# A mixture-of-experts tail whose weights are loaded once, kept in SBUF and copied to each tile by VectorE

## Chip, core and metric

The kernel runs on one core of one Trainium2 chip. The metric is the device time of one execution in microseconds (us), the median of three runs. The core's engines are named as in the profile: PE (TensorE matmuls), PEld (TensorE weight loads), DVE (VectorE), ACT (ScalarE), POOL (GpSimd), SP (SyncE, which here only issues DMAs).

## What is computed

Two layers of a hybrid vision network on an input of 2 images of 56 x 56 positions and 256 channels, all in float32. Layer 0 is a neighbourhood attention (7 x 7 window, 8 heads) behind a group norm. Layer 1 is a gated linear attention over the 3136 tokens of each image, followed by a mixture of experts. The mixture is the part that the change touches:

```python
xf = x.reshape(-1, 256)                          # 6272 tokens
probs = softmax(xf @ gate_w + gate_b)            # 8 experts
top2_vals, top2_idx = top_k(probs, 2)
cw = zeros((N, 8)); cw[arange(N)[:, None], top2_idx] += top2_vals
for e in range(8):                               # W1: 256 x 512, W2: 512 x 256
    h = gelu(xf @ W1[e] + b1[e])
    out += cw[:, e, None] * (h @ W2[e] + b2[e])
```

The kernel does not run every expert on every token. It sorts the 2 x 6272 pairs of token and expert by expert and runs each expert on its own tokens alone.

## The kernel before, in words

**Steps.** Layer 1 goes through the tokens in 13 steps (`NS1`) of 256 tokens of each image; the last step has 64. Three generators make a step: `before(s)` (projections and gates), `attention(s)` and, one step later, `route(s)`. `route(s)` normalises the result, computes the gate, finds each token's two experts and the slot of each pair, and scatters the token's row (256 channels, its number and its gate weights) into the DRAM buffer `xs_d`, which has one region per expert. It ends with `listed(s)`, which turns the counts into a list of full tiles: for each place its first row in `xs_d` and its expert, written as integers to a small tile `ent`. `together(main, *others)` interleaves the turns of these generators by fixed proportions.

**Places.** A place is one tile of slots of one expert. There are 57 of them (`NP`): 48 large ones of 256 slots and 9 small ones of 128. The first 41 (`sure1(NS1 - 2)`) are known to be full before the last step is routed. The last 16 are known only once `listed(NS1)` has run behind the last step; `places()` orders them as small and large in turn: S L S L S S L S L S S L S L S L. For each place `experts()` does the following.

- `fetch`: SP reads the place's row and expert from `ent` into registers (L1482), loads the slots `xg` from `xs_d` (L1492) and the expert's weights `wj` (128 partitions x 2308 floats, L1501) from DRAM.
- `gather`: DVE makes the row indices (`rowk`, L1514) and the gate weight of each slot (`cws`, L1522); PE transposes the slots (L1535), ACT copies them out (L1539).
- `hidden`: PE makes the hidden layer (`p_h`, L1550), ACT applies the gelu (`hT`, L1557).
- `results`: ACT writes the weighted bias to `ye` (L1569), PE makes the result (`p_y`, L1575), DVE adds the weighted result to `ye` (L1582), and POOL issues one indirect DMA per 128 slots that adds `ye` to the rows of `out` (L1585). Two places can hold rows of one token, so each place's adds wait until those of the place before have landed:

```python
before_it = added[-1] if added else []
...
waits_for(add, *before_it)
```

**Order.** In the steps the places run as one of the `others` of `together`, up to a bound `upto_k`; whatever is left runs behind the steps, in what is called the tail here. `ask` keeps the fetches ahead of the computing. In the steps a place's `xg` and `wj` lie in the pool `fw` of four buffers. When the steps' pools have been closed, the tail opens a second pool `tw` of four on their memory, uses both in turns of four, and lets the fetches run up to five places ahead. `fy` holds six buffers of `ye`. Within the order of priority the compiler places each engine's instructions by its own schedule, so that instructions of several generators stand mixed on an engine, and each engine then works through its own list in order.

Of the kernel before, what the change touches and what calls it, by code (L numbers as in the profile page):

```python
# [15 lines left out]
F32 = mybir.dt.float32  # L16
# [8 lines left out]
P = 128  # L25
# [23 lines left out]
NE, FF = 8, 512  # L49
# [8 lines left out]
RG = NB * L + SL  # L58
# [6 lines left out]
NS1 = -(-L // B1)  # L65
WJ = NG * FF + NF * C + NF + C
WP = 4
FW = 4
NW = 48
NO = 52  # L70
NP = 57
# [5 lines left out]
    return W, T, W // T  # L77


def places():  # L80

    first = sure1(NS1 - 2)
    large, small = iter(range(first, NW)), iter(range(NW, NP))
    return [*range(first), *(next(small if h else large) for h in (1, 0, 1, 0, 1, 1, 0, 1, 0, 1, 1, 0, 1, 0, 1, 0))]


def assigned(s):
    return 2 * NB * min((s + 1) * B1, L)


def sure1(s):
    return max(0, -((NE * (SL - 1) - assigned(s)) // SL))
# [717 lines left out]
def layer1(tc, t, out, x1_d, xs_d, ident, load, K, plain, lx, last_rows, lite):  # L810
    nc = tc.nc
# [11 lines left out]
    with ExitStack() as whole:  # L823
# [16 lines left out]
            pool = use.late if use.late is not None and n % 2 else p1  # L840
            return pool.tile(shape, F32, tag=tag, name=tag)

        use = SimpleNamespace(ahead=2, asked=0, tail=None, late=None)
        xin = {}

        def load_x(s):
# [17 lines left out]
        for what, shape, value in (  # L864
# [4 lines left out]
            first = const.tile(shape, F32, name=f"first_{what}")  # L869
# [575 lines left out]
        entry, added, puts, stores = [], [], {}, {}  # L1445
        fetched = {}
        order = places()
# [4 lines left out]
        def parts(k):  # L1452
            return 2 if order[k] < NW else 1

        def filled_at(k):
            return next((s for s in range(NS1) if sure1(s) > order[k]), NS1)

        def blank():
            for e in range(NE):
                row = nc.values_load(  # L1460
                    behind_[0:1, e : e + 1],
                    engines=[mybir.EngineType.SP],
                    min_val=e * RG,
                    max_val=e * RG + NB * L,
                    skip_runtime_bounds_check_because="an expert has at most K.every token",
                )
                put = nc.sync.dma_start(
                    out=xs_d[bass.ds(row, P), :], in_=empty[:, 0, :]
                )
                tc.declare_no_dep(put.ins, group="puts", reason="slots behind the last token")  # L1470
                tc.declare_no_dep(put.ins, group="gets", reason="full tiles are not written again")
                tc.add_to_no_dep_group("puts", put.ins)
                tc.add_to_no_dep_group(f"puts{NS1}", put.ins)
                puts.setdefault(NS1, []).append(put)

        def fetch(k, pool):
            n = parts(k)
            if filled_at(k) == NS1 and NS1 not in puts:
                blank()
            known = "the lists hold rows of the regions and experts alone"  # L1480
            row, exp = (
                nc.values_load(  # L1482
                    entry[order[k]][0:1, w, order[k] : order[k] + 1],
                    engines=[mybir.EngineType.SP],
                    min_val=0,
                    max_val=top,
                    skip_runtime_bounds_check_because=known,
                )
                for w, top in ((0, NE * RG), (1, NE - 1))
            )  # L1490
            xg = pool.tile([P, SL // P, ROW], F32, tag="xg", name="xg")
            get = nc.sync.dma_start(  # L1492
                out=xg[:, :n], in_=xs_d[bass.ds(row, n * P), :].rearrange("(u p) c -> p u c", p=P)
            )
            tc.add_to_no_dep_group("gets", get.ins)
            for earlier in range(filled_at(k) + 1):
                waits_for(get, *puts[earlier])
            for later in range(filled_at(k) + 1, NS1 + 1):
                tc.declare_no_dep(get.ins, group=f"puts{later}", reason="slots of later steps")
            wj = pool.tile([P, WJ], F32, tag="wj", name="wj")  # L1500
            nc.sync.dma_start(  # L1501
                out=wj.rearrange("p (n c) -> p n c", n=WP),
                in_=t["we_parts"][bass.ds(exp, 1)].rearrange("o n p c -> (o p) n c"),
            )
            fetched[k] = xg, wj

        def gather(k, pool, psum):
            xg, wj = fetched[k]
# [94 lines left out]
        done = [0]  # L1603

        def ask(k):
            while use.asked < k:
                n = use.asked
                fetch(n, use.w if use.tail is None or (n - use.tail) // FW % 2 else tw)
                use.asked += 1

        def experts():
            for k in range(NP):
                if use.tail is not None and k % 2 and use.ahead < 5:
                    use.ahead += 1
                ask(min(k + use.ahead + 1, len(entry)))
                if k == 0:
                    made = gather(0, use.x, use.psum)
                    yield
                wj = fetched[k][1]
                hT = yield from hidden(made[0], wj, use.x, use.psum)  # L1620
                if k + 1 < NP:
                    following = gather(k + 1, use.x, use.psum)
                    yield
                yield from results(k, hT, made, wj, use.x, use.psum)
                made = following
                fetched.pop(k)
# [24 lines left out]
        first, second, beside_it = before(0), before(1) if NS1 > 1 else iter(()), last_rows(ps_m)  # L1651
# [19 lines left out]
        for s in range(NS1 + 1):  # L1671
            others = []
            if s in beside_steps:
                n = -(-(all_beside - given) // (beside_steps[-1] - s + 1))
                others.append((islice(beside_it, n), n))
                given += n
            if s + 1 < NS1:
                others.append((before(s + 1) if s else second, n_before))
            if 0 < s < NS1:
                others.append((route(s - 1), n_route))  # L1680
            upto_k = max(0, (sure1(s - 2) if s > 1 else 0) - 1)
            if s == NS1:
                upto_k = min(upto_k, done[0] + 2)
            n = upto_k - done[0]
            if n > 0:
                others.append((until(upto_k), n * per_tile))
            if s < NS1:
                got = together((attention(s), n_att), *others)
                n_att = got if s == 0 else n_att
            else:  # L1690
                together((route(s - 1), n_route), *others)
            if s + 2 < NS1:
                load_x(s + 2)
            if s == beside_steps[-1]:
# [27 lines left out]
        listed(NS1)  # L1722
        steps.close()
        with (
            tc.tile_pool(name="tw", bufs=FW, reuse_waits="tile") as tw,
            tc.tile_pool(name="t_ps", bufs=8, space=PSUM, reuse_waits="tile") as ps_t,
            tc.tile_pool(name="tx", bufs=3, reuse_waits="tile") as tx,
        ):
            use.x, use.psum, use.tail = tx, ps_t, use.asked
            for _ in run:  # L1730
                pass

# [902 lines left out]
```

## Time and profile before

| | |
|---|---|
| median of 3 runs | 1440.71 us (1436.91 to 1442.93) |
| the profiled execution | 1438.56 us, of which span 1436.7 us |
| PE busy | 1270.4 us (88%) |
| PEld busy | 924.1 us (64%) |
| DVE busy | 791.0 us (55%) |
| ACT busy | 579.6 us (40%) |
| POOL busy | 469.6 us (33%) |
| DMA | 183.30 MB, mean 128 GB/s |
| weights `wj` | 57 loads of 1154.0 KB |
| the last matmul starts | 1405.57 us, a group of 16 that lasts 3.62 us |

The span runs from the first to the last instruction of the program. "Busy" is the union of an engine's instructions; waits, register loads and the issue of DMAs from SP are not counted. Where a line names what an engine waited for, that is the semaphore that came last by the profile.

### The profile page before, as it was taken

Reading aid. Unit: us, or ns where it says so; the run is one execution under the profiler, and the core shown is the slowest. Engines: PE = TensorE matmul, PEld = TensorE weight load, DVE = VectorE, ACT = ScalarE, POOL = GpSimd, SP = SyncE. Lnnn points to the kernel's source line nnn. Section 1 sums busy time; section 2 is a strip of 40 time slices with the busy share of each in tenths; the row PEclk is TensorE's granted clock in tenths of the full one; section 3 lists DMA queues with packets and bytes.
Section 4 is the critical chain, followed back from the end, with each engine's and each line's share of the span. In section 5 each row is a group of like instructions: output and inputs, shape, how many; then the busy total and the mean of one; then the engine's idle time right before and its main releaser. Section 6 shows DMA issues by size and latency. Waiting matters only on the chain. (4 is left out here: it accounts for less than half of the span.)

```text
span 1436.7 us, 29914 instructions
## 1 busy us (share of the span) xinstructions
PE 1270.4 (88%) x11566; PEld 924.1 (64%) x11566; DVE 791.0 (55%) x2694; ACT 579.6 (40%) x1053; POOL 469.6 (33%) x514
## 2 busy tenths in 40 slices
PE   2998999899899988779999999898999989989792
PEld 1566767676568664456767676666666677768681
DVE  7445556467675776665646465656564646441110
ACT  1443434444543523326453435343534353444240
POOL 0222223223113250432625242434343334442233
PEclk9999989999998989779999999999999999999996
DMA  9335344333123320315445344352626164489932
GB/s 284 116 107 159 110 145 133 103 109 110 33 56 100 101 82 23 102 41 192 138 120 155 96 131 124 97 158 64 190 55 188 46 195 134 141 214 360 326 34 31
DMA packets 122491, 183.30 MB, mean 128 GB/s; under 512 B 15628, under 2 KB 83724, under 8 KB 122340
## 3 DMA queue, kind: packets, MB, share of 16 engines
q1 hardware_dynamic: 90308, 129.05, 27.9%
q0 software_dynamic: 28864, 47.21, 14.3%
q10 hardware_dynamic: 3168, 5.05, 1.1%
q8 instruction: 93, 1.52, 0.4%
q14 instruction: 58, 0.48, 0.1%
HBM read 132.96 MB, written 48.27 MB: 126 GB/s over the span
## 5 line engine op out<-in xcount | busy, mean ns | idle before, releaser
L1585 POOL DMA_INDIRECT out<-ye,rowk x105 | 166.2, 1583 | 386.4 <-DVE ye L1582 134.5
L1575 PE MATMUL p_y<-wj,hT 128*128 128x256 f32 x840 | 216.4, 406 | 18.8 <-ACT hT L1557 12.8
L1550 PE MATMUL p_h<-xT_g,wj 128*128 128x256 f32 (+1 forms) x912 | 210.6, 370 | 3.4 <-issue 1.3
L1575 PEld LDWEIGHTS p_y<-wj,hT 128*128 128x128 f32 x840 | 163.9, 204 | 50.8 <-ACT hT L1557 15.0
L414 ACT ACTIVATE ex<-ex 98x1024 f32<-98x1024 f32 x98 | 103.6, 1057 | 208.6 <-DVE ex L408 201.4
L1550 PEld LDWEIGHTS p_h<-xT_g,wj 128*128 128x128 f32 x912 | 154.8, 190 | 29.0 <-issue 8.4
L1582 DVE SCALAR_TENSOR_TENSOR ye<-p_y,cws,ye 128x256 f32<-128x256 f32 x105 | 50.5, 481 | 161.9 <-PE p_y L1575 141.1
L408 DVE TENSOR_TENSOR ex<-sc,bias 98x1024 f32<-98x1024 f32 (+1 forms) x126 | 121.1, 978 | 33.4 <-PE sc L399 30.0
L1557 ACT ACTIVATE hT<-p_h,wj 128x256 f32<-128x256 f32 (+1 forms) x228 | 98.5, 452 | 90.6 <-PE p_h L1550 80.8
L399 PEld LDWEIGHTS sc<-qb,kc 64*98 64x98 f32 x1568 | 97.7, 171 | 50.3 <-issue 28.0
L399 PE MATMUL sc<-qb,kc 64*98 64x128 f32 x1568 | 122.1, 292 | 3.6 <-DVE slot L1323 1.1
L422 PE MATMUL po<-vw,ex 98*64 98x33 f32 x3136 | 118.5, 230 | 4.7 <-issue 2.3
L422 PEld LDWEIGHTS po<-vw,ex 98*64 98x64 f32 x3136 | 106.9, 145 | 21.9 <-issue 4.8
L1337 POOL DMA_INDIRECT xs_d<-xs,rowi x100 | 97.7, 977 | 70.8 <-DVE first L1379 30.6
L347 POOL TENSOR_TENSOR xo<-xo,xq 128x256 f32<-128x256 f32 x49 | 36.0, 734 | 243.9 <-DVE xo L341 226.2
L527 PE MATMUL pvv<-L_wvT,xs 128*112 128x256 f32 x224 | 62.6, 420 | 13.3 <-DVE top L519 13.3
L1569 ACT ACTIVATE ye<-wj,cws 128x256 f32<-128x256 f32 x105 | 50.1, 507 | 56.0 <-DVE own_e L1522 31.0
L1173 POOL TENSOR_TENSOR zc<-z,blk 128x256 f32<-128x256 f32 x48 | 34.2, 727 | 111.4 <-DVE z L1171 107.1
L994 DVE TENSOR_TENSOR pd<-p_u,k 128x512 f32<-128x512 f32 (+1 forms) x26 | 17.2, 660 | 96.6 <-PE pt_gate L1270 81.4
L1212 ACT COPY cT<-cx 128x256 f32<-128x256 f32 (+1 forms) x50 | 18.2, 364 | 124.9 <-PE p_h L1550 67.7
L349 POOL DMA_DIRECT2D x_d<-xo x98 | 56.8, 581 | 16.8 <-POOL xo L347 14.6
L1149 DVE TENSOR_TENSOR am<-sc,upto 128x512 f32<-128x512 f32 (+1 forms) x100 | 60.8, 668 | 0.8 <-PE sc L1140 0.6
(261 smaller groups left out, 2178.6 us busy)
## 6 DMA issues: line engine op xcount, KB each, us to landing
wj<-in_we_parts SPq DMA_DIRECT2D x57, 1154.0 KB
vw<-v_d SPq DMA_DIRECT2D x196, 101.1 KB
xg<-xs_d SPq DMA_DIRECT2D x48, 272.0 KB
v_d<-values POOLq DMA_DIRECT2D x28, 231.0 KB
xq<-in_x SPq DMA_DIRECT2D x98, 64.0 KB
x_d<-xo POOLq DMA_DIRECT2D x98, 64.0 KB
x_acc<-x_d SPq DMA_DIRECT2D x24, 256.0 KB
out<-x_acc POOLq DMA_DIRECT2D x24, 256.0 KB
```

The lines of the kernel that those rows point to most:

```text
L349: nc.gpsimd.dma_start(out=x1_d[b, i * QT : (i + 1) * QT, j * QT : (j + 1) * QT, :], in_=xo[b * QN : (b + 1) * QN, :],)
L399: nc.tensor.matmul(at[p][:KN, b, k], lhsT=keys(i, j, k, b, rows, g), rhs=qb[rows, g, :, b, j * QN : (j + 1) * QN], start=True, stop=True,)
L408: nc.vector.tensor_tensor(ex[:KN, of], sc[:KN].rearrange("n p b k h q -> n p b (k h q)"), bias[:KN, g, of].unsqueeze(2).to_broadcast([KN, ...
L414: nc.scalar.activation(ex[:KN], ex[:KN], AF.Exp)
L422: nc.tensor.matmul(po[b * QN : (b + 1) * QN, hh, :], lhsT=ex[:KN, h // 2, b, k, h % 2, :], rhs=vw[:KN, b, k, hh * (HD + 1) : (hh + 1) * (H ...
L527: nc.tensor.matmul(ps, lhsT=xs[:, b, k, j * TT : (j + 1) * TT], rhs=wv[:, k, :], start=k == 0, stop=k == NG - 1,)
L1149: nc.vector.tensor_tensor(am[:T, h, :, :, :T].rearrange("p b g t -> p (b g) t"), sc[:T, :, :, :T].rearrange("p b g t -> p (b g) t"), K.upt ...
L1337: put = nc.gpsimd.indirect_dma_start(out=xs_d[:, :], out_offset=bass.IndirectOffsetOnAxis(ap=rowi[:T, c, i : i + 1].bitcast(U32), axis=0), ...
L1550: nc.tensor.matmul(ph, lhsT=w1[:, k, f * P : (f + 1) * P], rhs=xT[:, k, :], start=k == 0, stop=k == NG - 1,)
L1557: nc.scalar.activation(hT[:, f, :], ph, AF.Gelu, bias=b1[:, f : f + 1])
L1575: nc.tensor.matmul(py, lhsT=hT[:, f, u * P : (u + 1) * P], rhs=w2[:, f, :], start=f == 0, stop=f == NF - 1,)
L1585: add = nc.gpsimd.indirect_dma_start(out=out[:, :], out_offset=bass.IndirectOffsetOnAxis(ap=rowk[:, u : u + 1].bitcast(U32), axis=0), in_= ...
```

## The change

The tail no longer loads weights for each place. Behind the steps it loads the weights of all eight experts once, into one tile `every_weight` of 8 x 2308 floats per partition on the memory that the steps had used (`tw`). The last 16 places fetch only their slots, into a pool `tg` of three; SP reads no expert for them. For each of them the new function `take` reads the expert into a register of VectorE and copies that expert's weights, in four pieces of 577 floats per partition, from `every_weight` into a `wj` buffer of the pool `fw`; the copy's source address comes from the register. `experts()` calls `take(k + 1)` at the start of place k, for the places 41 to 56.

Three smaller edits come with it. The bound on the places that run beside the steps now holds from the step before the last one on (`s >= NS1 - 1` in place of `s == NS1`): that step runs two places and not four. The tail's fetches run three ahead throughout, and `ask(done[0] + use.ahead)` issues those that can be known ahead of the loads of all weights. The tail's pool `tx` (`xT_g` and `hT`) has two buffers and not three.

```diff
+def listed_early():
+    return sure1(NS1 - 2)
...
-        def fetch(k, pool):
+        def weights(dst, src):
+            nc.sync.dma_start(
+                out=dst.rearrange("p (n c) -> p n c", n=WP), in_=src.rearrange("o n p c -> (o p) n c")
+            )
+
+        def listed_for(k, what, engine):
+            return nc.values_load(
+                entry[order[k]][0:1, what, order[k] : order[k] + 1],
+                engines=[engine],
...
+        def fetch(k):
             n = parts(k)
+            late = k >= listed_early()
+            pool = use.rows if late else use.w
             if filled_at(k) == NS1 and NS1 not in puts:
                 blank()
...
+            row = listed_for(k, 0, mybir.EngineType.SP)
+            exp = None if late else listed_for(k, 1, mybir.EngineType.SP)
             xg = pool.tile([P, SL // P, ROW], F32, tag="xg", name="xg")
...
-            fetched[k] = xg, wj
+            wj = None
+            if not late:
+                wj = pool.tile([P, WJ], F32, tag="wj", name="wj")
+                weights(wj, t["we_parts"][bass.ds(exp, 1)])
+            fetched[k] = [xg, wj]
+
+        def take(k):
+            exp = listed_for(k, 1, mybir.EngineType.DVE)
+            wj = fetched[k][1] = use.w.tile([P, WJ], F32, tag="wj", name="wj")
+            for n in range(WP):
+                part = slice(n * WJ // WP, (n + 1) * WJ // WP)
+                nc.vector.tensor_copy(
+                    wj[:, part], use.all[:, bass.ds(exp, 1), part].rearrange("p o c -> p (o c)")
+                )
...
         def ask(k):
             while use.asked < k:
-                n = use.asked
-                fetch(n, use.w if use.tail is None or (n - use.tail) // FW % 2 else tw)
+                fetch(use.asked)
                 use.asked += 1
 
         def experts():
             for k in range(NP):
-                if use.tail is not None and k % 2 and use.ahead < 5:
-                    use.ahead += 1
                 ask(min(k + use.ahead + 1, len(entry)))
+                if listed_early() <= k + 1 < NP:
+                    take(k + 1)
...
-            if s == NS1:
+            if s >= NS1 - 1:
                 upto_k = min(upto_k, done[0] + 2)
...
-            tc.tile_pool(name="tw", bufs=FW, reuse_waits="tile") as tw,
+            tc.tile_pool(name="tw", bufs=1, reuse_waits="tile") as tw,
             tc.tile_pool(name="t_ps", bufs=8, space=PSUM, reuse_waits="tile") as ps_t,
-            tc.tile_pool(name="tx", bufs=3, reuse_waits="tile") as tx,
+            tc.tile_pool(name="tx", bufs=2, reuse_waits="tile") as tx,
+            tc.tile_pool(name="tg", bufs=3, reuse_waits="tile") as tg,
         ):
-            use.x, use.psum, use.tail = tx, ps_t, use.asked
+            use.x, use.psum, use.rows, use.ahead = tx, ps_t, tg, 3
+            ask(done[0] + use.ahead)
+            use.all = tw.tile([P, NE, WJ], F32, name="every_weight")
+            for e in range(NE):
+                weights(use.all[:, e], t["we_parts"][e : e + 1])
             for _ in run:
                 pass
```

More of the change, by code (lines that the diff above doesn't have):

```diff
@@ L77, in size @@
     return W, T, W // T
+def listed_early():
+    return sure1(NS1 - 2)
 def places():
-    first = sure1(NS1 - 2)
-    large, small = iter(range(first, NW)), iter(range(NW, NP))
-    return [*range(first), *(next(small if h else large) for h in (1, 0, 1, 0, 1, 1, 0, 1, 0, 1, 1, 0, 1, 0, 1, 0))]
+    large, small = iter(range(listed_early(), NW)), iter(range(NW, NP))
+    return [*range(listed_early()), *(next(small if h else large) for h in (1, 0, 1, 0, 1, 1, 0, 1, 0, 1, 1, 0, 1, 0, 1, 0))]
 def assigned(s):
@@ L841, in either @@
             return pool.tile(shape, F32, tag=tag, name=tag)
-        use = SimpleNamespace(ahead=2, asked=0, tail=None, late=None)
+        use = SimpleNamespace(ahead=2, asked=0, late=None)
         xin = {}
@@ L1474, in blank @@
                 puts.setdefault(NS1, []).append(put)
-        def fetch(k, pool):
+        def weights(dst, src):
[6 more added lines that the diff above has]
+                engines=[engine],
+                min_val=0,
+                max_val=(NE * RG, NE - 1)[what],
+                skip_runtime_bounds_check_because="the lists hold rows of the regions and experts alone",
+            )
+        def fetch(k):
             n = parts(k)
+            late = k >= listed_early()
+            pool = use.rows if late else use.w
             if filled_at(k) == NS1 and NS1 not in puts:
                 blank()
[L1480 to L1490, printed above, removed]
+            row = listed_for(k, 0, mybir.EngineType.SP)
+            exp = None if late else listed_for(k, 1, mybir.EngineType.SP)
             xg = pool.tile([P, SL // P, ROW], F32, tag="xg", name="xg")
@@ L1499, in fetch @@
                 tc.declare_no_dep(get.ins, group=f"puts{later}", reason="slots of later steps")
[L1500 to L1504, printed above, removed]
-            fetched[k] = xg, wj
+            wj = None
[10 more added lines that the diff above has]
+                    wj[:, part], use.all[:, bass.ds(exp, 1), part].rearrange("p o c -> p (o c)")
+                )
         def gather(k, pool, psum):
```

## The prediction, made before the changed kernel was run

> **What bounds the kernel now.** The page's chain of waits covers only the last few per cent, so I asked three narrower views of the tail: busy time by stretch, the groups of instructions from 1290 us on, and the timeline of POOL, ACT and PE.
>
> First the stretches (length, busy time of each engine, PE clock, DMA share, GB/s):
>
> ```profile
> 1299.00:1366.00 67.00, 57.85 (x310) 50.84 (x308) 10.40 (x53) 25.27 (x68) 18.70 (x13) 0.96 1.00 336
> 1366.00:1423.00 57.00, 43.04 (x226) 38.12 (x226) 7.81 (x36) 17.68 (x48) 22.98 (x15) 0.86 0.32 36
> ```
>
> From 1299 to 1366 us the DMA engines are full (share 1.00): these are the weights. Behind that they are nearly idle, and so, a third of the time, is PE. Something else paces the end. The groups name it:
>
> ```profile
> L1585 POOL DMA_INDIRECT out<-ye,rowk x30 | 46.3, 1544 | 91.5 <-DMA out<-ye,rowk 81.3 <-DVE own_e L1522 6.3 <-issue 2.4
> ```
>
> POOL's adds to `out` wait 81.3 us for the adds before them to land: they are a serial chain. Its starts:
>
> ```profile
> 1299.31 1.54 POOL L1585 DMA_INDIRECT out<-ye,rowk  x1 [7.91 <-DMA out<-ye,rowk]
> ...
> 1309.03 1.54 POOL L1585 DMA_INDIRECT out<-ye,rowk  x1 [6.33 <-DMA out<-ye,rowk]
> ...
> 1365.84 1.54 POOL L1585 DMA_INDIRECT out<-ye,rowk  x1 [8.14 <-DMA out<-ye,rowk]
> ...
> 1396.51 1.54 POOL L1585 DMA_INDIRECT out<-ye,rowk  x1 [2.91 <-DMA out<-ye,rowk]
> ...
> 1423.03 1.54 POOL L1585 DMA_INDIRECT out<-ye,rowk  x1 [2.90 <-DMA out<-ye,rowk]
> 1424.88 1.54 POOL L1585 DMA_INDIRECT out<-ye,rowk  x1 [0.30 <-issue]
> ```
>
> Counting back 30 adds, 1299.31 is place 38, 1365.84 place 45, 1423.03 place 56. A large place takes the chain 9.7 us while weights stream (1299.31 to 1309.03) and 6.4 us when they don't (1385.64 to 1392.06); a small one 7.8 and 4.5. PE makes a large and a small place in 11.08 us (1379.96 to 1391.04), a large one in 7.35 (1246.66 to 1254.01), a small one behind a small one in 3.73. So the quiet chain (10.9 for the pair) just keeps up with PE, the loaded one does not. It falls behind until all six `ye` buffers are taken, and then ACT and PE stand:
>
> ```profile
> 1345.96 0.51 ACT L1569 ACTIVATE ye<-wj,cws 128x256 f32<-128x256 f32 x1 [6.03 <-DMA out<-ye,rowk]
> ...
> 1365.23 0.51 ACT L1569 ACTIVATE ye<-wj,cws 128x256 f32<-128x256 f32 x1 [9.47 <-SPq L700]
> 1366.15 6.30 PE L1575 MATMUL p_y<-wj,hT 128*128 128x256 f32 x16 [6.24 <-ACT hT L1557]
> ```
>
> (The second releaser is a mere neighbour in time; 1365.23 is the landing of the adds issued at 1356.) The end is thus set by the chain: 5 large and 2 small places in 66.5 us, then 7 small and 4 large in 57.2, then 13.7 us from 1423.03 to the end of the span.
>
> **What the Trainium skill says.** (1) "VectorE: DVE Perf Modes", the perf-mode tier table: an fp32 copy between SBUF addresses runs at two elements a cycle, 2048 elements in 1227 ns. The trace agrees with two: 448 elements from SBUF take 503 ns, from PSUM 743.
>
> ```profile
> L269 DVE TENSOR_SCALAR xs<-xs,gm,gr 128x448 f32<-128x448 f32 x28 | 13.3, 503 | 7.9 <-DMA xs<-in_xT 7.8
> L305 DVE TENSOR_SCALAR qb<-pq,bq,slot_of 128x448 f32<-128x448 f32 x28 | 20.8, 743 | 34.8 <-ACT qb L302 34.7
> L889 DVE TENSOR_SCALAR root_a<-ve x26: 155/170/4375, 358.2 to 1241.2; 128x4 int32<-128x4 int32 x24, 64x2 int32<-64x2 int32 x2
> ```
>
> (2) "SBUF — State Buffer", "SBUF: two separate sides": such a copy and a GpSimd instruction lock each other out of a shared port; an indirect DMA's descriptors are then late. The third line above agrees from DVE's side: an operation of 170 ns took 4375 once, beside a POOL addition of 2.9 us. Beside the adds it is mild: `rowk` (L1514) rises from some 160 ns to 425 at most. (3) "DMA: Bandwidth & Descriptors", "SWDGE vs HWDGE vs iDMA": each DMA engine takes turns between POOL's queue and SP's. That fits adds that wait 6 to 8 us behind weights and 2.9 without.
>
> **The change, part by part.**
>
> *Weights.* 17 loads go out from 1289.21 on, one per place 40 to 56, the last at 1356.27, in 1154 KB each. They become 8 loads, and those of place 40 and probably 39: 10. With some 3.6 MB of slots the 17 made about 324 GB/s, so 8 loads (9.45 MB) take 29 us and ten about 36. They need no list, but their memory is the steps': I take it that they start when the list is done (1290 before), since the listing's tiles lie under them. Both ends: some start up to 8 us earlier, or none runs faster than 275 GB/s (17 loads in 73 us by themselves), 34 us for eight.
>
> *Two places out of the second last step.* Places 34 and 35 held PE from 1246.66 to 1267.12, 20.5 us, 14.7 of it work and the rest stalls. They now come behind the list. Without them the last route's transposes (1268.99) and the list come earlier. Against it, attention and route of that step lose cover: between 1218.7 and 1241 PE had 11.6 us of places and would have 4.3; the route's own chain is then about 17 us long in 22. I take 4 us of the 20.5 as lost and 16 as the shift: list at 1274, place 36 in PE at 1270, its first add at 1299.3 - 16 = 1283.3. Bounds 12 and 20.
>
> *The chain then.* Weights stream to about 1310. Three large places at 9.7 (36 to 38) and two at 6.4 make 41.9; places 41 to 55, nine small at 4.5 and six large at 6.4, 78.9. First add of place 56: 1283.3 + 41.9 + 78.9 = 1404.1. Before: 1423.03.
>
> *PE then.* From 1270 without a stall: 5 x 7.35 + 85 (seven pairs at 11.08 and two small at 3.73) = 1392. But weights of 39 can stand in SP's queue behind the eight: 1274 + 29 + 4 = 1307, where PE wants them at 1292. Then 1307 + 2 x 7.35 + 85 = 1407 is PE's end, its first add of place 56 at 1405. Both limits agree within 2 us; I take 1405. The first `take` waits for all eight loads (1303) and is wanted at about 1320: hidden.
>
> *The copies.* 64 copies of 577 floats. From the tier table's 1227 ns for 1024 cycles, an estimate of 0.46 us at two a cycle and 0.76 at one. Register loads are 16 on DVE; SP's (L1482) have median 0.27 and maximum 0.41. A place costs DVE 4 x 0.46 + 0.3 = 2.1 us. For a large and a small place DVE does 2.7 us now (three `ye` at 0.48, `rowk`, five or so small ones) and then 7 of 11.08: hidden behind PE. In DVE's queue a copy stands ahead of some `ye`, by at most 2.1 us; the adds that want that `ye` are late already. What is not hidden is the port: each place's adds can meet a copy in flight. Not shown in this trace; from nothing to all four copies (1.8 us); I take 0.3 a place, 15 places, 4.5 us on the chain.
>
> *At nothing:* SP's 16 expert reads fall away and the tail's slots come three ahead through three buffers (SP idle); `tx` of two holds, since the steps ran with two (`fx`).
>
> *Sum:* 1405 + 4.5 + 13.7 = 1423 against a span of 1436.7, so 14 us less. Outside the span lie 1.9 us (1438.56). The median of the runs, 1440.71, is 2.15 above the profiled one, so I forecast 1426.5.
>
> **The rivals.**
>
> - *The loads come early.* If the eight wait each for their own piece of memory alone, streaming ends at about 1295. Then the chain has one loaded place, and the add of 36 does not wait behind a loaded one of 35 either, 4 us: 1279 + 9.7 + 4 x 6.4 + 78.9 = 1393, PE's end 1392: a median near 1411. For it: DMA share is 0.60 from 1246 to 1267 us, there is room. Against: the listing writes into a large steps' tile to the end.
> - *The loads block.* At 275 GB/s (34 us), the loads of 39 and 40 behind them (8 us) and DVE standing at the first `take` with `ye` behind it, place 39 begins at 1274 + 42 = 1316; first add of 56 at 1316 + 14.7 + 85 - 2 = 1414, with the port 1418, median 1436. No change that a measurement can tell from none.
> - *VectorE becomes the bound.* The pair leaves (10.9 - 3.3) / 8 = 0.95 us per copy before DVE is slower than the chain. If copies with a register's address wait for POOL and cost 1.3 us, the pair takes 3.3 + 8 x 1.3 = 13.7, 8 pairs lose 22 us against the 14 gained, and the kernel ends 8 us later than before; from there on it is slower. At 1.5: 35 us lost, median about 1462. For it: the 4375 ns line. Against: adds hold up `rowk` by 0.27 us at most.
> - *It doesn't do what it says:* no; the last 16 loads are gone by construction.
>
> **How the numbers follow.** Forecast (gains of 8 to 24 us) 0.62; early loads 0.13; blocking 0.16; VectorE 0.09. Half a per cent, 7.2 us, is about what a measurement of this kernel can tell from no change. Faster: 0.62 + 0.13 + a fifth of the third, 0.78; same 0.13; slower 0.09. The range 1411 to 1438 takes in early loads and blocking and leaves the last out. The shift of 12 to 20 us and a port cost of 0 to 13 lie within it.
>
> **What would show it.** Right: 49 loads of `wj` (41 and 8), adds in the last 50 us 4.5 and 6.4 us apart, no `ye` on ACT that waits for an add, copies of 0.4 to 0.8 us on DVE, DMA quiet from about 1310. Wrong: PE idle of over 20 us for `wj`; adds at over 1.8 us on POOL or copies at over 1 us (the port); a list later than 1280 (lost cover). The forecast falls if the chain is loaded for more than five places.

## The result, and the profile after

| | before | after |
|---|---|---|
| median, chip of the prediction (20 runs each) | 1435.92 us | 1428.03 us |
| ratio of the runs | | 0.9934, 95% interval 0.9912 to 0.9956 |
| profiled execution, span | 1436.7 us | 1427.0 us |
| PE busy | 1270.4 us | 1268.5 us |
| DVE busy | 791.0 us | 814.2 us |
| DMA | 183.30 MB | 173.87 MB |

The kernel is 7.9 us faster; 14.2 were forecast. Of these 6.3 us that are missing 4.8 lie in the base: the 20 runs of the kernel before have a median 4.8 us below that of the three runs that the prediction started from. Between the two profiled spans 9.7 us were gained and 13.7 forecast.

The list of DMA issues after shows that the change does what it says, 41 loads of weights for the places and 8 for all experts:

```profile
wj<-in_we_parts SPq DMA_DIRECT2D x41, 1154.0 KB
every_weight<-in_we_parts SPq DMA_DIRECT2D x8, 1154.0 KB
```

The stretches of the tail after (length; busy time of PE, PEld, DVE, ACT, POOL; PE clock; DMA share; GB/s):

```profile
1274.00:1316.00 42.00, 28.98 (x131) 24.10 (x130) 7.84 (x36) 12.15 (x27) 12.39 (x8) 0.84 0.99 324
1316.00:1343.00 27.00, 27.00 (x148) 24.26 (x147) 14.28 (x55) 13.23 (x32) 11.58 (x8) 1.00 0.49 87
1343.00:1413.00 70.00, 66.57 (x380) 59.95 (x378) 26.87 (x90) 30.66 (x76) 27.89 (x18) 1.00 0.41 62
```

The DMA engines were full for 67 us of the tail before (336 GB/s); now they are for 42 us (324), with 62 to 87 GB/s behind that. From 1316 us on PE has no idle time at all (the 66.57 us end at 1409.57 with its last matmul); before, it idled for a quarter of the last 57 us. The price stands in the first line: PE works 29 of 42 us while the eight loads stream. The timelines of SP, PE and DVE show that price in detail:

```profile
1272.53 0.41 SPq L1480 DMA_DIRECT2D wj<-in_we_parts  x1
1278.56 17.11 SPq L1480 DMA_DIRECT2D every_weight<-in_we_parts  x8
1296.20 4.23 SPq L1502 DMA_DIRECT2D xg<-xs_d  x1
```

```profile
1311.72 1.11 PE L1553 MATMUL pt_g<-ident,xg 128*128 128x128 f32 x4 [12.82 <-DMA xg<-xs_d]
```

```profile
1311.35 1.20 DVE L1521 COPY wj<-every_weight 128x577 f32 x3 [15.31 <-DMA every_weight<-in_we_parts]
```

The weights of place 39 still go ahead of the eight. The slots of place 40 go out behind them, at 1296.20, and arrive only with the last of them at 1311.7. PE transposes a place's slots ahead of the second product of the place before, so place 39's results stand as well. DVE has stood since 1296 at its first `take`, which waits for all eight loads: its source can lie in any of them.

POOL's adds, the line that carried the prediction (start, duration, what the queue waited for; a large place has two adds, of which the first is shown, from place 37 to 41 and then 55 and 56):

```profile
1290.62 1.54 POOL L1603 DMA_INDIRECT out<-ye,rowk  x1 [6.44 <-DMA out<-ye,rowk]
...
1300.22 1.54 POOL L1603 DMA_INDIRECT out<-ye,rowk  x1 [6.21 <-DMA out<-ye,rowk]
...
1316.73 1.54 POOL L1603 DMA_INDIRECT out<-ye,rowk  x1 [13.12 <-DVE ye L1600]
...
1323.86 1.54 POOL L1603 DMA_INDIRECT out<-ye,rowk  x1 [3.74 <-DVE ye L1600]
...
1331.02 1.54 POOL L1603 DMA_INDIRECT out<-ye,rowk  x1 [3.66 <-DMA out<-ye,rowk]
...
1408.53 1.54 POOL L1603 DMA_INDIRECT out<-ye,rowk  x1 [3.09 <-DVE ye L1600]
1413.10 1.54 POOL L1603 DMA_INDIRECT out<-ye,rowk  x1 [3.03 <-DMA out<-ye,rowk]
```

Up to 1300 us a large place takes 9.6 us as before, then 16.5 at the stall above. From place 41 on the first adds of a small place and the next are 4.5 to 4.8 us apart, of a large one and the next 6.4 to 7.5.

Executions differ by several us in parts that no edit here touches. To compare single profiles I therefore count from a landmark ahead of all edits, the first add of place 29 (1188.75 us before, 1191.08 after), and split the way from there to the end at place 41, the first of the last 16. (All landmark figures are from one profile of each kernel.)

| kernel | 29 to 41 | 41 to 56 | 29 to the end of the span |
|---|---|---|---|
| before | 139.7 | 94.6 | 247.9 |
| after | 139.9 | 82.1 | 235.9 |

**The whole gain, 12 us here, lies behind place 41**, where the adds no longer share the DMA engines with weights. Up to place 41 nothing was gained, although the list is ready 16 us earlier (1273.9 us on the clock of the trace, 1289.9 before; 18 us by the landmark).

### The profile page after: what moved, and what is told of

It is laid out like the page before. It is cut to its first block, busy times and chain, and to the rows that moved or that the text cites. A ratio compares the mean times of both kernels' runs of the same rounds, so it can differ in the third digit from the quotient of the medians.

```text
span 1427.0 us, 29974 instructions
## 1 busy us (share of the span) xinstructions
PE 1268.5 (89%) x11566; PEld 923.6 (65%) x11566; DVE 814.2 (57%) x2758; ACT 583.7 (41%) x1053; POOL 470.7 (33%) x514
## 2 busy tenths in 40 slices
DMA packets 118270, 173.87 MB, mean 122 GB/s; under 512 B 15500, under 2 KB 83596, under 8 KB 118116
## 4 chain that ended last, share of the span: by engine, by line
PE 41%; DVE 12%; ACT 3%; DMA 3%; issue 2%; SPq 1%; POOL 1%; another core or an unknown queue 0%; ACTq 0%; DVEq 0%; POOLq 0%
PE p_y L1593 11%; PE p_h L1568 9%; PE p_qkv L968 7%; PE p_out L1221 3%; PE cx L1203 2%; PE pt_g L1553 1%; PE p_u L990 1%; PE p_sum L1005 1%; SPq L1480 1%; PE cx L1190 1%; ACT xs L926 1%; PE pt_x L940 1%; DMA xg<-xs_d 1%; DVE root L895 1%; DVE am L1152 1%
## 5 line engine op out<-in xcount | busy, mean ns | idle before, releaser
L1593 PE MATMUL p_y<-wj,hT 128*128 128x256 f32 x840 | 211.5, 400 | 6.1 <-DVE am L1152 5.9
L1575 ACT ACTIVATE hT<-p_h,wj 128x256 f32<-128x256 f32 (+1 forms) x228 | 100.8, 454 | 104.5 <-PE p_h L1568 94.6
L997 DVE TENSOR_TENSOR pd<-p_u,k 128x512 f32<-128x512 f32 (+1 forms) x26 | 17.2, 661 | 97.1 <-PE pt_gate L1273 81.9
L1203 PE MATMUL cx<-am,kp 128*32 128x128 f32 (+1 forms) x800 | 55.9, 301 | 6.7 <-issue 3.7
```

The source lines that it names most:

```text
L1203: nc.tensor.matmul(cx[hp, g, :T], lhsT=kp[:T, b, g, hp], rhs=am[:T, h, b, g, :T], start=False, stop=True,)
L1575: nc.scalar.activation(hT[:, f, :], ph, AF.Gelu, bias=b1[:, f : f + 1])
L1593: nc.tensor.matmul(py, lhsT=hT[:, f, u * P : (u + 1) * P], rhs=w2[:, f, :], start=f == 0, stop=f == NF - 1,)
```

## The experiments

The theory after this reading: the gain is the quiet chain of adds; what is missing of the forecast is the standstill at places 39 and 40 behind the eight loads. The rivals: the earlier list is the gain; PE's waits for `ye` buffers were; or the copies hold the tail back. The runs were made on three chips. On one of them the kernel before takes 1436.14 us, as on the chip of the prediction (1435.92; whether it is the same one is not on record). On the two others it takes 1386.40 and 1383.82. So ratios to the kernel before on the same chip are compared, and landmark figures only among chips at 1436 us or among chips at 1385. Of the kernel before there is no profile from a chip at 1385 us. On these two chips the changed kernel itself measured 0.9902 (0.9871 to 0.9932; 1372.9 us against 1386.4) and 0.9908 (0.9879 to 0.9938; 1371.15 against 1383.82): 13 us faster.

> The changed kernel once more, as the measure for the three runs beside it. Both theories: some 0.993 of the kernel before, place 40 about 14 us late on PE because its slots queue behind the eight loads, the chain of adds from place 40 to place 56 about 89 us.

> The changed kernel again, as the measure on this chip for the three beside it: 0.990 to 0.994 of the kernel before, place 41 some 50 to 56 us behind the list's end.

The ratios are a little lower than the 0.993 expected. On PE place 41 started 55.7 and 53.6 us behind the end of the list, in the expected span. Place 40 started 28.2 and 26.2 us behind place 39, that is 19 to 21 us late with 7.35 for the work, where 14 were expected. The chain from 40 to 56 took 89.1 and 87.6 us.

### One part alone: two places moved

```diff
-            if s == NS1:
+            if s >= NS1 - 1:
```

> The kernel before with one part of the change alone: two places move out from beside the last list to behind it. My theory: the list ends about 16 us earlier, but the weights still stream behind it and the chain of adds, at 9.7 us a large place while they do, sets the end: within 3 us of the kernel before. Rival (the two places are most of the gain): 5 to 8 us faster, a ratio of 0.994 to 0.996.

Measured, on the chip at 1436 us: ratio 1.0004 (0.9982 to 1.0025). Counted from place 29, the list was ready 85.3 us later and not 101.2, 16 us earlier than in the kernel before, and nothing came of it: the adds took 144.0 us to place 41 instead of 139.7 and 90.1 from there to 56 instead of 94.6. Two more places stand in the loaded chain instead. The rival's ratio of 0.994 to 0.996 lies outside the interval: the earlier list is no gain by itself.

### The other part alone: the weights kept, the two places left where they were

```diff
-            if s >= NS1 - 1:
+            if s == NS1:
```

> The changed kernel, but with two more places ahead of the last list, as before the change. My theory: the list ends near 1290 instead of 1274, the eight loads end near 1328 instead of 1311, and place 41 starts 8 to 10 us later on the clock of places though two more places are done by then: PE stands about as long as now, so within 4 us of the changed kernel. Rival (moving the two places out is the gain by itself): back to the time of the kernel before, 8 us slower than the changed one.

Measured, on a chip at 1385 us: 0.9958 (0.9939 to 0.9977; 1381.2 us), so 5 us faster than the kernel before and 8 slower than the changed one. Mine missed by 4 us; the rival has the 8, but not the return to the kernel before. The profiled execution is one of the fastest of the 22 (1374.62 us), but counted from place 29 it too ends 4.8 us later than the mean of the two profiles of the changed kernel here. Its chain of adds shows where:

```profile
1250.04 1.54 POOL L1603 DMA_INDIRECT out<-ye,rowk  x1 [6.28 <-DMA out<-ye,rowk]
...
1269.95 1.54 POOL L1603 DMA_INDIRECT out<-ye,rowk  x1 [16.52 <-DVE ye L1600]
```

These are places 39 and 40. The loads start at 1234.5 instead of 1223 and land at 1264.6. With two places fewer left over, the chain has run out of results by 1250 and stands for 16.5 us: place 40's second product waits on PE behind the transposes of 41, whose slots stand behind the eight. So the two places are worth nothing as a shift of the list, but they are work for the chain while the eight loads stream. (The median lies some 3 us further off than this profile. Over the 22 executions the time goes with the mean granted clock of PE, about 1 us for 0.001. The median of that clock is 0.9425 here and 0.9455 in the changed kernel beside it. Whether the clock is the cause of these 3 us, or is lower because PE stands longer, the runs don't show.)

### More buffers for the kernel before

```diff
-for n, k in (("fs", 8), ("fx", 2), ("fy", 6), ("fw", FW))
+for n, k in (("fs", 8), ("fx", 2), ("fy", 8), ("fw", FW))
```

> The kernel before with eight buffers for the experts' results instead of six. My theory: PE and ScalarE stand less for a buffer, but the chain of adds ends no earlier: within 2 us of the kernel before. Rival (PE's standstill for buffers, 6.2 and 2.4 us, is on the path): 4 to 8 us faster.

Measured, on the chip at 1436 us: 0.9985 (0.9955 to 1.0016). The stretches of this run, at the times that the prediction showed of the kernel before:

```profile
1299.00:1366.00 67.00, 67.00 (x385) 60.69 (x384) 12.45 (x64) 30.12 (x80) 18.54 (x12) 1.00 0.98 325
1366.00:1423.00 57.00, 29.40 (x158) 26.03 (x156) 5.66 (x25) 11.89 (x30) 23.14 (x15) 0.80 0.34 39
```

PE no longer stands in the first stretch (67.00 us of work instead of 57.85) and, counted from place 29, begins its last place 202.8 us on instead of 213.4. Of these 10.6 us the end shows 3.7 (244.2 for 247.9), the medians 2.8. That lies between the two expectations, within 2 us and 4 to 8, and the interval allows both. What decides is the profile: PE ran 10.6 us ahead and two thirds of that were lost again behind the chain of adds. PE's waits for buffers were mostly the chain's effect. (PE's granted clock in the first stretch rose from 0.96 to 1.00 with this. A higher clock for PE alone would thus have met the same bound.)

### The traffic put back

```diff
+            if late:
+                behind(weights(use.again[k % 2], t["we_parts"][k % NE : k % NE + 1]), get)
+            else:
...
+            use.again = [td.tile([P, WJ], F32, name=f"again{i}") for i in range(2)]
```

(`td` is a pool in DRAM; the load stands on SP's queue behind the slots of its place.)

> The changed kernel, with weights loaded once more behind each late place's slots into scratch memory that nobody reads, so that DMA is as full in the tail as before the change. My theory (the gain is that the adds land sooner when no weights stream): the chain takes 9 to 10 us again for a large place and 7 to 8 for a small one while they stream, and the kernel ends 10 to 25 us later than the changed one, at the time of the kernel before or behind it. Rival (the gain comes from PE not waiting for weights or from VectorE's copies being at hand): less than 4 us slower.

Measured, on a chip at 1385 us: 1.025 (1.0216 to 1.0284), 47 us slower than the changed kernel beside it. The direction is as by my theory, the size nearly twice its upper end. The stretches and the adds:

```profile
1250.00:1300.00 50.00, 38.76 (x184) 32.40 (x185) 17.54 (x67) 14.03 (x36) 13.60 (x9) 0.91 1.02 243
1300.00:1345.00 45.00, 34.73 (x182) 29.99 (x181) 16.27 (x60) 13.70 (x39) 11.29 (x7) 0.89 0.92 218
```

```profile
1283.20 1.54 POOL L1605 DMA_INDIRECT out<-ye,rowk  x1 [8.53 <-DMA out<-ye,rowk]
1293.86 1.54 POOL L1605 DMA_INDIRECT out<-ye,rowk  x1 [9.12 <-DMA out<-ye,rowk]
...
1307.39 1.75 POOL L1605 DMA_INDIRECT out<-ye,rowk  x1 [10.15 <-DMA out<-ye,rowk]
```

With the DMA engines full again (a share of 0.92 to 1.02) a small place takes 10.7 us and a large one 13.5, not 4.5 and 6.4. What POOL waited for, here from 1250 us on and in the first profile of the changed kernel from 1317 on:

```profile
L1605 POOL DMA_INDIRECT out<-ye,rowk x29 | 45.6, 1573 | 113.0 <-DMA out<-ye,rowk 100.0 <-DVE ye L1602 6.4 <-DVE own_e L1542 4.1
```

```profile
L1603 POOL DMA_INDIRECT out<-ye,rowk x27 | 42.6, 1576 | 70.3 <-DMA out<-ye,rowk 38.2 <-DVE ye L1600 26.4 <-DVE own_e L1540 3.3
```

Of its 113.0 us of waiting 100.0 are for the adds before, and only 10.5 for results or slots. PE stands too, but from 1260 us on only 2.2 us of that are for slots; 24.8 are for ScalarE, which itself waits 40.6 us for `ye` buffers that the adds hold and 27.9 for the gate weights that DVE makes from the slots. So the chain leads, and the late slots reach it for 10.5 us at most. It is slower here than it was before the change (7.8 and 9.7). One difference is that each load here ends in DRAM and not in SBUF; no run shows that this is the reason. That adds wait while another queue has packets on the same engines fits what the Trainium skill states in "DMA: Bandwidth & Descriptors", "Queues, rings and completion order": each DMA engine goes round the queues that it has work for, a packet at a time.

### The copies twice

```diff
-            for n in range(WP):
+            for n in (0, 0, 1, 1, 2, 2, 3, 3):
```

> The changed kernel with every copy of a late place's weights made twice, the second to the same place. My theory: VectorE has room (some 1.6 to 1.9 us of copies in 4 to 7 us a place), so only the port that it shares with GpSimd and the first place behind the loads pay: 1 to 4 us slower than the changed kernel. Rival (VectorE and the port are the bound of the tail): 1.65 us for each of 16 places, 20 to 26 us slower.

Measured, on the same chip: 0.9945 (0.9922 to 0.9968), against 0.9908 for the changed kernel: 1377.73 us and 1371.15. By the ratios 5 us slower, by the medians 6.6, with intervals that overlap; the rival's 20 to 26 are excluded. How much of the 5 to 7 us the copies cost is open: five of the 16 executions took 1367.5 to 1372.0 us at mean granted clocks of 0.947 to 0.953, no more than the changed kernel beside it at 0.947 and 0.948 (1368.3 to 1371.9). The other eleven took 1376.7 to 1383.0 at 0.939 to 0.946, and two of the changed kernel 1375.1 and 1375.5 at 0.941 and 0.942. The profile is of one of the five. The groups of DVE in the tail, the changed kernel's first (from 1317 us) and then this run's (from 1262 us):

```profile
L1521 DVE COPY wj<-every_weight 128x577 f32 x56 | 22.9, 470 | 0.6 <-issue 0.2
```

```profile
L1521 DVE COPY wj<-every_weight 128x577 f32 x104 | 40.9, 465 | 0.7 <-issue 0.3
```

A copy takes no longer when there are twice as many. On POOL some adds do:

```profile
1269.64 2.90 POOL L1603 DMA_INDIRECT out<-ye,rowk  x1 [3.37 <-DVE wj L1521]
```

One took 2.90 us, several 1.72 to 1.83, against 1.54 undisturbed. The chain from place 41 to 56 took 82.8 us, hardly more than the changed kernel's 80.1 and 82.0. VectorE and the port have room.

### Where does the standstill come from, and is it lost time?

Five orders of the same transfers. First, place 40's slots and weights ahead of the eight:

```diff
-            ask(done[0] + use.ahead)
+            ask(listed_early())
...
-                weights(use.all[:, e], t["we_parts"][e : e + 1])
+                behind(weights(use.all[:, e], t["we_parts"][e : e + 1]), use.last)
```

> Place 40's slots and weights go on SP's queue ahead of the eight loads. My theory (the standstill at places 40 and 41 is lost time that only the start of the tail decides): place 40 starts at about 1303 instead of 1317, place 41 waits for its copies until about 1317 instead of 1325, and all behind it comes 7 us earlier; 5 to 7 us faster than the changed kernel, the first add of place 56 at about 1406. Rival (the chain of adds, slowed by the copies, sets the end whatever PE does): less than 2 us.

Measured: 0.9889 (0.9859 to 0.992), 1372.21 us beside the changed kernel's 1372.9: less than 2 us, as the rival had it. The wait only moved, from place 40's slots to place 41's:

```profile
1261.69 0.69 PE L1553 MATMUL pt_g<-ident,xg 128*128 128x128 f32 x2 [12.91 <-DMA xg<-xs_d]
```

Then two loads at the list's end, place 40's weights, and six more (`begin` issues the first two, in `fetch` ahead of place 40's weights; the other six stand behind those; the second line keeps the last step's `xs` from lying under `every_weight`):

```diff
-            pool = use.late if use.late is not None and n % 2 else p1
+            pool = use.late if use.late is not None and n % 2 == (tag != "xs") else p1
...
+            if k == listed_early() - 1:
+                use.begin()
...
+            for e in range(2, NE):
+                behind(weights(use.all[:, e], t["we_parts"][e : e + 1]), use.last)
```

> Two of the eight loads, then place 40's weights, then the other six; place 40's slots ahead of all; and the step's slot tiles swap places, so that the room of the eight loads does not wait for the last scatter. My theory: the loads begin at about 1274 instead of 1278.6 and have landed by about 1310, PE never stands for more than 3 us there, place 41 starts at about 1312 instead of 1325; 9 to 12 us faster than the changed kernel, unless the chain of adds becomes the bound first: from place 40's first add at about 1310 its 89 us give 1399 for place 56, 14 us earlier than 1413. Rival (the chain is paced by the copies, or by the loads under way): no more than 3 us faster than with the slots ahead alone.

Measured: 0.9905 (0.9874 to 0.9936). The first two loads went out at 1218.38, as soon as the list was done, but place 40's weights waited for their buffer until 1224.26 and the six stood behind them; the copies began at 1257.6 and place 41 again waited for its slots (12.0 us). My 9 to 12 us did not come.

Then, in the first of these orders, the slots of 41 to 43 ahead as well:

```diff
-            ask(done[0] + use.ahead)
+            ask(listed_early() + use.ahead)
...
+            if late:
+                use.last = get
```

> As with the slots ahead, and the slots of places 41 to 43 ahead of the eight loads too. My theory after the last runs (place 41's slots, whose transposes PE does ahead of place 40's second product, took over as the wait when place 40's went ahead): place 40's second product no longer stands, place 41 starts as soon as its copies are made, 2 to 4 us behind the landing of the eight loads and about 5 us earlier than with place 40's slots alone ahead; 4 to 6 us faster than the changed kernel, a ratio of 0.986 to 0.987. Rival (the landing of the eight loads alone sets the end, whatever stands ahead): the ratio stays at 0.989 to 0.991.

Measured, on the chip at 1436 us: 0.9904 (0.9868 to 0.9939), where the changed kernel has 0.9934 (0.9912 to 0.9956) on the chip of the prediction: not told apart, and short of the 0.986 to 0.987 of my theory. And both together, the last diff on top of the second order:

> Both at once: two of the eight loads at the list's end, with the slot tiles swapped so that their room is free, then place 40's weights, the slots of 41 to 43, then six loads. My theory: the loads land 2 to 3 us earlier than in the run beside it, place 41 starts 7 to 9 us earlier than in the changed kernel; 6 to 9 us faster, a ratio of 0.984 to 0.986. Rival (the landing of the loads does not move, since the last six wait for the last scatter as before): as the run beside it, within 2 us.

Measured, on the same chip: 0.9925 (0.9904 to 0.9946), no better, where 0.984 to 0.986 were expected. Slots of 41 wait for the blank rows of the last step to land (on SP in both runs for 2.2 us or more) and the loads wait behind them: here the last six went out at 1290.0, 20 us behind the list. In the run with all eight behind the slots, PE then waited for the copies alone:

```profile
1328.38 3.75 PE L1570 MATMUL p_h<-xT_g,wj 128*128 128x128 f32 x16 [9.95 <-DVE wj L1523]
```

while its chain of adds ran on without a gap, at its loaded pace (places 37, 38, 39 and 40, first adds):

```profile
1300.96 1.54 POOL L1605 DMA_INDIRECT out<-ye,rowk  x1 [6.00 <-DMA out<-ye,rowk]
...
1310.78 1.54 POOL L1605 DMA_INDIRECT out<-ye,rowk  x1 [6.42 <-DVE ye L1602]
...
1320.42 1.54 POOL L1605 DMA_INDIRECT out<-ye,rowk  x1 [6.25 <-DMA out<-ye,rowk]
...
1328.83 1.77 POOL L1605 DMA_INDIRECT out<-ye,rowk  x1 [5.02 <-DVE wj L1523]
```

That suggested the opposite of my theory: PE's standstill is covered by a chain that is late already. The last run takes nearly all of the standstill away. Blanks first, five loads at the list's end, place 40's weights, three loads, with the steps' slot tiles swapped as before; the late places' slots on ScalarE's queue:

```diff
-            row = listed_for(k, 0, mybir.EngineType.SP)
+            row = listed_for(k, 0, mybir.EngineType.Activation if late else mybir.EngineType.SP)
...
-            get = nc.sync.dma_start(
+            get = (nc.scalar if late else nc.sync).dma_start(
...
+            def begin():
+                blank()
+                for e in range(5):
+                    use.fifth = weights(use.all[:, e], t["we_parts"][e : e + 1])
+                    behind(use.fifth, puts[NS1][-1])
```

> The blanks first, five of the eight loads at the list's end (slot tiles swapped, so that their room is free), place 40's weights, three more loads, and the slots of the late places on ScalarE's queue, where they stand behind no load. My theory (the tail starts when the bulk of nine loads has landed, some 35 us behind the list, and every earlier order only moved the wait from one thing to another): the copies of place 41 start at 35 to 38 us behind the list's end instead of 37 to 41, place 41 follows within 4 us instead of 13, PE stands about 3 us there, and the kernel is 6 to 10 us faster than the changed one. Rival (the chain of adds, 89 us from place 40 to 56 whatever starts it, is held by its own waits, or slot loads on ScalarE's queue cost what they save): within 3 us of the changed kernel.

Measured: 0.9887 (0.9856 to 0.9918), 1370.6 us beside the changed kernel's 1371.15: as the rival had it. The copies began 43.0 us behind the list, later than expected and than in the changed kernel beside it (40.7), but place 41 followed within 0.7 us and not 12.9:

```profile
1258.63 3.23 PE L1572 MATMUL p_h<-xT_g,wj 128*128 128x128 f32 x16 [3.39 <-DVE wj L1525]
```

PE's wait behind the loads fell from 17.1 us (in the changed kernel beside it, for slots) to 3.4, with 3.3 more at place 37, where ScalarE stood for the scatters before it could issue slots. Place 41 started 11.5 us earlier, counted from place 29 (117.9 us against 129.4). The end came 2.6 us earlier by the same count, and the medians differ by 0.6. The stretch from 1257 to 1345 us, first of this run, then of the changed kernel:

```profile
1257.00:1345.00 88.00, 82.56 (x462) 74.06 (x463) 40.39 (x147) 40.32 (x100) 36.38 (x23) 0.98 0.42 67
```

```profile
1257.00:1345.00 88.00, 88.00 (x499) 79.55 (x498) 40.80 (x146) 43.06 (x105) 35.18 (x22) 0.99 0.44 75
```

PE, ahead now, idles 5.4 us of the 88: it is no longer the one that is waited for. The table by landmark, chips at 1385 us (the changed kernel twice, once on each):

| kernel | 29 to 41 | 41 to 56 | 29 to the end |
|---|---|---|---|
| changed | 136.3, 138.2 | 82.0, 80.1 | 232.7, 232.0 |
| slots of 40 first | 136.1 | 80.2 | 230.3 |
| two, then six | 136.0 | 82.1 | 232.1 |
| own queue | 133.6 | 82.1 | 229.4 |
| two places kept | 141.4 | 81.9 | 237.2 |
| copies twice | 136.6 | 82.8 | 233.1 |
| traffic put back | 146.7 | 115.4 | 275.8 |

Place 41 to 56 takes 80 to 83 us in every kernel with a quiet tail, whichever way it is begun, on chips at 1436 us too (82.1 to 82.3). In the three kernels that load weights for each place it takes 90.1 to 94.6. None of the other orders beats the changed kernel by more than the runs can tell, and I have no version that does.

## Why the prediction was right, and where its steps were off

**The mechanism holds.** Chain of adds, slow while weights stream and quick when they don't: shown by the traffic put back (the chain from 40 to 56 takes 127 us, not 88, and waits for its own adds) and by the buffers (PE 10.6 us earlier, the end 3.7). All that the prediction named as signs is there: 49 loads; the spacing of the adds; no `ye` on ACT waiting for an add; copies of 0.44 to 0.64 us, median 0.454, as the estimate from the tier table of "VectorE: DVE Perf Modes" in the Trainium skill had it (0.46 at two elements a cycle, 0.76 at one). The trace of the kernel before, which the prediction read as agreeing with two, did not decide it: worked out in the same way, 448 elements take an estimated 0.39 us at two and 0.63 at one, and the 503 ns lie between. DMA is quiet from about 1316 on, though less so than behind the last weights before (share 0.41 to 0.49, against 0.32).

**Its sum, term by term.**

| term | predicted | measured |
|---|---|---|
| list ready | 1274 | 1273.9 |
| first add of 36 | 1283.3 | 1280.79 |
| 36 to 41 | 41.9 | 50.2 |
| 41 to 56, with the port | 78.9 + 4.5 | 82.1 |
| last place's first add to the end | 13.7 | 13.9 |

The term that was mis-sized is the third, 8.3 us too short in this profile; on the chips at 1385 us it measured 43.0 and 44.0. "The first `take` waits for all eight loads (1303) and is wanted at about 1320: hidden" failed in both halves: the loads landed at 1311, and DVE came to the `take` at 1296, since place 41's copies stand in its list behind the results of place 38. The prediction did see a stall behind the eight loads, "weights of 39 can stand in SP's queue behind the eight", and timed PE's return at 1307. What stood there were the slots of place 40, four of PE's transposes, and through PE's order the results of 39 with them; PE returned at 1311.7. That they start 4.6 us behind the list was missed too: SP waited for the last scatter, whose source tile lies under `every_weight`:

```profile
SPq L1480 <- DMA xs_d<-xs,rowi: 5.4, 1, 5.4
```

**Two limits that agree.** The prediction had the chain at 1404 and PE at 1405 for place 56. The orders of the loads agree with that: on the chips at 1385 us, where the chain from 36 to 41 took 43 and 44 us, PE's standstill of 17 us cost next to nothing, and taking it away moved the bound to the chain. In the profile from the prediction's chip the same stall did hold the chain (13.12 us at place 39); by the landmark the two reordered kernels on the chip at 1436 us end 2.7 us earlier and 3.5 us later than the changed one (the later profile is of the slowest of nine executions), so the runs don't show it as loss either. My first reading, which took the standstill for the missing gain, fell. From place 41 on both limits bind in the changed kernel: PE has no idle time, and the chain still waits mostly for its own adds (38.2 us from 1317 us on, for results 13.3 without the stall at place 39).

**The shift of the list.** "16 as the shift" was right as a time (16.0) and yielded nothing by itself: two places more in the loaded chain cost what the earlier list gave. In the prediction's own sum it brought little either: place 41 came at 1325.2 against 1328.4 before. What the two places do bring, cover for the chain while the loads stream (some 5 us by the landmark, 8 by the medians), was not seen.

**What was luck.** The forecast of 1426.5 us lies 1.5 us from the measured median, which is closer than its steps were. The span came out at 1427.0 us and not at 1423. Against that, the median was forecast 2.15 us above the profiled execution and lay 0.75 below it. The forecast also stands 0.7 us below its own sum: 1405 + 4.5 + 13.7 is 13.5 us less than the span of 1436.7, and 13.5 off 1440.71 gives 1427.2. One reading of the stretches was off as well: between 1366 and 1423 us PE idled a quarter of the time (43.04 of 57 us busy), not a third.

**The rivals.** Loads come early: no, they wait for the list and a scatter. VectorE the bound: no, even doubled copies cost at most 5 to 7 us. Loads block: in its kind it came, slots behind the loads and DVE at the first `take`, but with place 39 begun at 1295 and PE back at 1311.7, where it had place 39 begin at 1316. The first add of 56, at 1413.1, lies between the forecast's 1409.5 and this rival's 1418.

## What to carry to other kernels

Where a serial chain of small transfers sets the end, count the bulk traffic beside it first: here, moving nine megabytes out of its way gained what neither more buffers, nor an earlier list, nor an earlier PE could. A standstill of the busiest engine is worth only what the next limit leaves, so ask how far behind the chain is before mending it. And a bulk transfer placed ahead of small ones on one queue holds up whatever is issued behind it; if work for the other engines is left over at that point, put it there.

## What the hardware showed that I had not expected

- Loads held the queue that issued them while much was in flight: eight of 1154 KB took 17.11 us to issue on SP, the first four in 2.4 us and then 3.1 to 4.5 us each. The next, small, load was out 17.6 us behind the first of the eight.
- Copies with a source address from a register were no slower than the estimate at two elements a cycle (median 0.454 us for 577 elements, estimate 0.46).
- VectorE's copies cost POOL's adds less than the 4.5 us that the prediction took for the port: adds of 1.54 us became 1.65 to 1.77 now and then, and 27 of them from 1317 us on took 42.6 us, a mean of 1.576, which is 1 us more in all. This doesn't speak against the exclusive lock that the Trainium skill states in "SBUF — State Buffer", "SBUF: two separate sides": no add grew by more than 0.23 us, half of one copy, and with the copies doubled one grew by 1.36, the length of three.
- The waits of the chain behind other traffic depend on more than the share of busy DMA engines: at a share of 1.00 it took 9.7 us a large place beside loads into SBUF, and at 0.92 to 1.02 it took 13.5 beside loads into DRAM. The rate was lower beside these (218 to 243 GB/s, not 336).
